# A spectral block with a 3x3 convolution: four rows from six products, a refined inverse root on GpSimd, a table of free PSUM banks and new order lists

## Chip, cores and metric

The kernel runs on one core of one Trainium2 chip. The metric is the device time of one execution in microseconds (us), as the median over runs. All data are fp32.

## What is computed

The input `x` is four images of 256 x 256 positions with 64 channels. Layer 0 normalises it over the channels, applies a spectral step (2-D FFT, a 256 x 256 mixing matrix with GELU, inverse FFT, projection), adds the result to `x`, and then does a second normalisation, a 64 to 128 projection, a depthwise 3x3 convolution, GELU and a 128 to 64 projection. Layer 1 replaces the sequence by its moving average plus a filtered rest, which the kernel does as one 256 x 256 matrix for each channel.

```python
h = _pw(_ln(x, g1, b1), w_te, b_te)
F = jnp.fft.fft2(h.astype(jnp.complex64), axes=(1, 2))
fr = jnp.concatenate([jnp.real(F), jnp.imag(F)], axis=-1)
fc = jax.nn.gelu(_pw(fr, w_fc, b_fc), approximate=False)
re, im = (fc[..., :HID], fc[..., HID:])
sp = jnp.real(jnp.fft.ifft2(re + 1j * im, axes=(1, 2)))
x1 = x + _pw(sp, w_tp, b_tp)
h2 = _pw(_ln(x1, g2, b2), w_fe, b_fe)
d = lax.conv_general_dilated(h2, w_dw, window_strides=(1, 1), padding='SAME',
                             dimension_numbers=('NHWC', 'HWIO', 'NHWC'), feature_group_count=HID) + b_dw
d = jax.nn.gelu(d, approximate=False)
return x1 + _pw(d, w_fp, b_fp)
```

## The kernel before

The kernel is one program with an order written out by hand for TensorE (PE), VectorE (DVE), ScalarE (ACT) and GpSimd (POOL). Every operation has a short name. Lists such as `FULL` and `SPECTRUM` say which operations one period `n` issues and for which index: `cf0:-3` is `cf0` for the chunk of three periods ago. `FOLLOWS` names what each operation needs before it, and `do` issues missing predecessors first. The queue SP holds nearly all DMAs, in an order that the framework derives.

There are five kinds of stages.

- The first (`FIRST`, `BETWEEN`) transforms columns of `x` along the height (`forward_h`) and builds layer 1's matrices.
- The second (`SPECTRUM`) goes on with the forward transform and does the spectral step, two pairs of frequency blocks in a period (`x`, `xs`, `m0`, `m1`, `gc`, `b`, `g`, `p`, `z`, `zs`, `w`, `zt`) and the inverse transform along the width (`u`, `us`, `uc`, `uf`).
- Then `FULL` adds one convolution chunk to each period. A chunk is 8 of 256 columns of one image, so there are 32 chunks for each image and 128 in all. While the forward transform still has chunks (it ends at period 127), such a period holds forward, spectral and convolution work. Later it holds spectral and convolution work, and for the last image convolution alone.
- Last comes layer 1, one 256 x 256 matrix product for each channel over all images (L1200), evicted by DVE and ACT in turns (L1214, L1212).

A convolution chunk goes like this. `s` finishes the inverse FFT (L833); `r0`, `r1` add it to `x` (L846, L853); `cq`, `cr`, `cR`, `cm`, `cM`, `cp` make the inverse norm (`statistics`, L192 to L233): the sum (L213), the squares on ACT (L210), minus the mean's square (L217), the sum of squares (L220), their sum (L224), and the power -1/2 on GpSimd (L230). `cx` scales (L237), `t` transposes to channels (L870), `tt` evicts (L878). `T0`, `T1` form sums of rows on GpSimd (L890 to L895): this is the fast algorithm for a 3-tap filter that gets two output rows from four products. `gm`, `gh` and `em`, `eh` make these products on PE: `wc_main` for two neighbouring columns at once (L916) and `wc_half` for the third (L935), into banks of 512 columns, one for each product and column parity. `gc_`, `cf`, `ce` put the products together into two rows (L955 to L967), `cE` corrects the image's edges (L974 to L980), `a` is the GELU (L984), `o` the projection (L991), `fs`, `ft`, `st` turn it back and add it to `x1` (L1002 to L1026).

PSUM banks come from one pool of eight in rotation (`bank`, L141): the n-th tile gets the bank of the tile eight places before it.

The lines that carry the algorithm for two rows:

```python
if i:
    even, odd = by_row(1)[:, 0], by_row(1)[:, 1]
    nc.gpsimd.tensor_tensor(td[:, 0], odd, even, ALU.add)
    nc.gpsimd.tensor_tensor(td[:, 1], odd, even, ALU.subtract)
    ks = (1, 2)
else:
    for r in range(2):
        nc.gpsimd.tensor_tensor(td[:, r], by_row(0)[:, r], by_row(2)[:, r], ALU.subtract)
    ks = (0, 3)
```

Of the kernel before, what the change touches and what calls it, by code (L numbers as in the profile page):

```python
# [11 lines left out]
F32 = mybir.dt.float32  # L12
AF = mybir.ActivationFunctionType
ALU = mybir.AluOpType
# [4 lines left out]
P = 128  # L19
N = 256  # L20
# [4 lines left out]
NPOS = float(N * N)  # L25

# [10 lines left out]
def _tables():  # L37
# [4 lines left out]
    fold = lambda m: m.reshape(2, P, -1).transpose(1, 0, 2).reshape(P, -1)  # L42

# [8 lines left out]
    ihi[0] = 0.5 * cos[P, :P] / NPOS  # L52

# [8 lines left out]
    icr[0] *= 0.5  # L62

# [5 lines left out]
    first = np.maximum(off_h, (dx == 0)[:, None])  # L69
    last = np.maximum(off_h, (dx == 2)[:, None])  # L70
    rows = off_h[:, [0, N - 1] * 4]
    edge = np.zeros((P, 2 * N + 8))
# [21 lines left out]
    for par in range(2):  # L94
# [20 lines left out]
        "avgT": fold(avg.T),  # L115
# [14 lines left out]
def conv_seq_kernel(ctx: ExitStack, tc: tile.TileContext, a: dict, tables: bass.AP, out: bass.AP):  # L130
# [5 lines left out]
    psum = ctx.enter_context(tc.tile_pool(name="psum", bufs=8, space=PSUM))  # L136
# [4 lines left out]
    def bank(name):  # L141
        return psum.tile([P, 512], F32, tag="bank", name=name)
# [42 lines left out]
    wc_main = const([P, 2, 4, HID], "wc_main")  # L185
    wc_half = const([P, 4, HID], "wc_half")
# [3 lines left out]
    edge_rows = const([P, 4, 2], "edge_rows")  # L190

    def statistics(pool, index, src, name):  # L192

        state = {}

        def get(j):
            if j not in state:
                n = src(j).shape[1]
                state[j] = [
                    pool.tile([P, n], F32, tag=tag, name=f"{tag}_{name(j)}", bufs=bufs)  # L200
                    for tag, bufs in (("total", 2), ("squares", 2), ("var", 3))
                ]
            return state[j]

        squares = {}

        def square(j):
            n = src(j).shape[1]
            squares[j] = shared.tile([P, n, C], F32, tag="sq", name=f"sq_{name(j)}")
            nc.scalar.activation(squares[j], src(j), AF.Square)  # L210

        def add(j):
            nc.vector.tensor_reduce(get(j)[0], src(j), AX.X, ALU.add)  # L213

        def less_mean(j):
            total, _, var = get(j)
            nc.vector.scalar_tensor_tensor(var, total, -1.0 / C, total, ALU.mult, ALU.mult)  # L217

        def add_squares(j):
            nc.vector.tensor_reduce(get(j)[1], squares.pop(j), AX.X, ALU.add)  # L220

        def variance(j):
            _, total, var = get(j)
# [147 lines left out]
    def forward_h(pool):  # L371
# [73 lines left out]
        def evict(j, m):  # L445
# [12 lines left out]
            if out[j] < 2:  # L458
                return
# [983 lines left out]
```

## Time and profile before

| | us |
|---|---|
| median of 3 runs | 4445.63 |
| lowest, highest | 4442.97, 4450.9 |
| span of the profiled execution | 4447.0 |
| granted TensorE clock, mean | 0.993 |
| DVE busy in that span | 3561.7 |
| GpSimd busy | 2774.3 |
| ScalarE busy | 2505.2 |

The profile counts from the first to the last instruction. Its page gives the busy time of each engine; the costliest groups by line, engine, operation and tile follow with count, busy time, mean time of one, and the idle time ahead of them. These are some of the groups:

```profile
L594 POOL TENSOR_TENSOR g<-g 128x512 f32<-128x512 f32 (+1 forms) x520 | 736.2, 1429 | 520.9 <-ACT g L588 520.9
L916 PE MATMUL ps_h_c<-td_c,wc_main 128*128 128x512 f32 x2048 | 921.7, 593 | 0.0
L230 POOL TENSOR_TENSOR rstd_c<-var_c,minus_half 128x16 f32<-128x16 f32 x128 | 371.8, 2905 | 468.1 <-DVE var_c L224 457.4
L935 PE MATMUL ps_h_c<-td_c,wc_half 64*128 64x128 f32 (+1 forms) x4032 | 515.3, 392 | 4.3 <-POOL td_c L890 4.3
L967 DVE TENSOR_TENSOR h_c<-h_c,ps_h_c 128x512 f32<-128x512 f32 x512 | 317.3, 682 | 125.8 <-PE ps_h_c L935 125.7
```

Busy time is a union, so a matmul's mean of 593 ns with 450 ns busy each means that neighbours overlap in the pipeline. The two passes of one fp32 product are counted as two instructions.

### The profile page before, as it was taken

Reading aid. Unit: us, or ns where it says so; the run is one execution under the profiler, and the core shown is the slowest. Engines: PE = TensorE matmul, PEld = TensorE weight load, DVE = VectorE, ACT = ScalarE, POOL = GpSimd, SP = SyncE. Lnnn points to the kernel's source line nnn. Section 1 sums busy time; section 2 is a strip of 40 time slices with the busy share of each in tenths; the row PEclk is TensorE's granted clock in tenths of the full one; section 3 lists DMA queues with packets and bytes.
Section 4 is the critical chain, followed back from the end, with each engine's and each line's share of the span. In section 5 each row is a group of like instructions: output and inputs, shape, how many; then the busy total and the mean of one; then the engine's idle time right before and its main releaser. Section 6 shows DMA issues by size and latency. Waiting matters only on the chain.

```text
span 4447.0 us, 63373 instructions
## 1 busy us (share of the span) xinstructions
PE 4346.2 (98%) x22379; PEld 2219.4 (50%) x22379; DVE 3561.7 (80%) x5473; ACT 2505.2 (56%) x3694; POOL 2774.3 (62%) x1774
## 2 busy tenths in 40 slices
PE   7899999799999999999999999999999999999999
PEld 4444443355555555455555555555555455554444
DVE  7979999899999999999998777777778788872222
ACT  2338888666666666666666666666664343431121
POOL 6869998887777777777777555555554555530000
PEclk9999999899999999999999999999999999999999
DMA  6665556444444444444444343333334433329996
GB/s 189 201 191 143 156 156 176 133 114 133 133 133 133 133 128 138 119 133 133 133 133 119 105 114 95 101 104 100 95 104 126 145 105 94 90 59 373 345 346 231
DMA packets 757733, 655.01 MB, mean 147 GB/s; under 512 B 40269, under 2 KB 651551, under 8 KB 749096
## 3 DMA queue, kind: packets, MB, share of 16 engines
q1 hardware_dynamic: 720552, 583.82, 44.3%
q10 hardware_dynamic: 36864, 67.13, 3.9%
q8 instruction: 179, 2.93, 0.3%
q14 instruction: 138, 1.13, 0.1%
HBM read 364.81 MB, written 286.00 MB: 146 GB/s over the span
## 4 chain that ended last, share of the span: by engine, by line
PE 88%; DVE 5%; POOL 2%; DMA 2%; issue 1%; ACT 1%; SPq 1%; ACTq 0%; DVEq 0%; POOLq 0%
PE ps_h_c L916 19%; PE ps_h_c L935 11%; PE ps_p L565 10%; PE ps_o L1200 9%; PE ps_z L618 5%; PE ps_u L667 5%; PE ps_f_c L991 5%; PE ps_x L541 5%; PE ps_s_c L833 5%; PE ps_y L436 4%; PE ps_ft_c L1012 3%; PE ps_t_c L870 3%; PE ps_zt L635 2%; DMA out_dram<-oc 1%; PE ps_m L1120 1%
## 5 line engine op out<-in xcount | busy, mean ns | idle before, releaser
L594 POOL TENSOR_TENSOR g<-g 128x512 f32<-128x512 f32 (+1 forms) x520 | 736.2, 1429 | 520.9 <-ACT g L588 520.9
L916 PE MATMUL ps_h_c<-td_c,wc_main 128*128 128x512 f32 x2048 | 921.7, 593 | 0.0
L584 DVE TENSOR_TENSOR g<-ps_p,g 128x512 f32<-128x512 f32 x1040 | 692.9, 682 | 30.4 <-ACT g L579 12.4
L588 ACT ACTIVATE g<-g,b_fc 128x1024 f32<-128x1024 f32 (+1 forms) x520 | 586.5, 1148 | 180.3 <-DVE g L584 177.8
L230 POOL TENSOR_TENSOR rstd_c<-var_c,minus_half 128x16 f32<-128x16 f32 x128 | 371.8, 2905 | 468.1 <-DVE var_c L224 457.4
L579 ACT COPY g<-ps_p 128x512 f32<-128x512 f32 (+1 forms) x520 | 302.0, 582 | 453.3 <-PE ps_p L565 438.8
L916 PEld LDWEIGHTS ps_h_c<-td_c,wc_main 128*128 128x128 f32 x2048 | 369.1, 190 | 369.8 <-issue 303.0
L935 PEld LDWEIGHTS ps_h_c<-td_c,wc_half 64*128 64x128 f32 x4032 | 417.0, 187 | 244.4 <-issue 194.4
L565 PE MATMUL ps_p<-xs,wp 64*128 64x512 f32 (+1 forms) x2080 | 519.0, 603 | 6.3 <-ACT xs L556 6.3
L935 PE MATMUL ps_h_c<-td_c,wc_half 64*128 64x128 f32 (+1 forms) x4032 | 515.3, 392 | 4.3 <-POOL td_c L890 4.3
L1200 PE MATMUL ps_o<-xc,mt 128*128 128x512 f32 x1024 | 439.9, 592 | 1.3 <-DVE oc L1214 1.3
L230 POOL TENSOR_TENSOR rstd<-var,minus_half 128x16 f32<-128x16 f32 x128 | 384.6, 3005 | 87.5 <-DVE var L224 87.5
L967 DVE TENSOR_TENSOR h_c<-h_c,ps_h_c 128x512 f32<-128x512 f32 x512 | 317.3, 682 | 125.8 <-PE ps_h_c L935 125.7
L984 ACT ACTIVATE h_c<-h_c,b_conv 128x1024 f32<-128x1024 f32 x256 | 280.7, 1147 | 200.6 <-DVE h_c L980 200.5
L1214 DVE TENSOR_SCALAR oc<-ps_o,b_fp 128x512 f32<-128x512 f32 x128 | 93.2, 749 | 345.4 <-DMA out_dram<-oc 181.1
L430 POOL TENSOR_TENSOR xb<-xt 128x512 f32<-128x512 f32 x224 | 288.3, 1305 | 91.9 <-DVE xt L423 89.9
L960 DVE TENSOR_TENSOR h_c<-h_c,ps_h_c 128x512 f32<-128x512 f32 x256 | 175.7, 686 | 202.0 <-PE ps_h_c L935 193.5
L1200 PEld LDWEIGHTS ps_o<-xc,mt 128*128 128x128 f32 x1024 | 194.4, 190 | 246.1 <-issue 236.1
L541 PEld LDWEIGHTS ps_x<-tab,yb 128*64 128x64 f32 x4064 | 241.9, 138 | 129.8 <-issue 91.6
L618 PE MATMUL ps_z<-g,w_tp 128*64 128x512 f32 x1024 | 281.9, 613 | 22.2 <-POOL g L594 21.0
L1212 ACT ACTIVATE oc<-ps_o,b_fp 128x512 f32<-128x512 f32 x128 | 85.9, 686 | 356.6 <-PE ps_o L1200 171.0
L436 PE MATMUL ps_y<-xb,tab 128*64 128x512 f32 x1024 | 257.1, 609 | 28.8 <-POOL xb L430 28.0
(144 smaller groups left out, 7676.8 us busy)
## 6 DMA issues: line engine op xcount, KB each, us to landing
y_d<-yt SPq DMA_DIRECT2D x256, 256.0 KB, 2.5
yb<-y_d SPq DMA_DIRECT2D x256, 256.0 KB, 3.7
u_d<-ut SPq DMA_DIRECT2D x256, 256.0 KB, 4.1
x_c<-in_x_dram SPq DMA_DIRECT2D x128, 512.0 KB, 5.6
x_d<-st SPq DMA_DIRECT2D x128, 512.0 KB, 4.8
xc<-x_d SPq DMA_DIRECT2D x64, 1024.0 KB, 8.6
out_dram<-oc ACTq DMA_DIRECT2D x256, 256.0 KB, 6.0
xt<-in_x_dram SPq DMA_DIRECT2D x504, 128.0 KB, 2.7
```

The source lines that it names most:

```text
L230: nc.gpsimd.tensor_tensor(rstd, var, minus_half.to_broadcast([P, n]), ALU.pow)
L436: nc.tensor.matmul(ps[i * C : (i + 1) * C], dh[:, m, i * C : (i + 1) * C], sums[j][:, i], start=True, stop=True,)
L541: nc.tensor.matmul(ps[r * C : (r + 1) * C, j * N + t * P : j * N + (t + 1) * P], blk[:, t, k, r * C : (r + 1) * C], tb[:, t, :], start=Tru ...
L565: nc.tensor.matmul(ps[:, :nf], wp[rows, cols], rhs[rows], start=True, stop=r == 1 or not pr["special"],)
L584: nc.vector.tensor_tensor(gt[:, i], re, gt[:, 1], op)
L588: nc.scalar.activation(g, g, AF.Gelu, bias=b_fc[:, half : half + 1])
L594: nc.gpsimd.tensor_tensor(g[:, 0], g[:, 0], g[:, 1], op)
L618: nc.tensor.matmul(ps[r * C : (r + 1) * C, :nf], w_tp, d[:, :nf], start=True, stop=True)
L916: nc.tensor.matmul(ps, wc_main[:, par, k, :], ts[(*j, k)].rearrange("p j i -> p (j i)"), start=True, stop=False,)
L935: nc.tensor.matmul(pss[k, par][:, s * P : (s + n) * P], wc_half[lo : lo + C, k, :], ts[(*at_q, k)][lo : lo + C, at : at + n, :].rearrange( ...
L967: nc.vector.tensor_tensor(g, g, m, (ALU.add, ALU.subtract)[r])
L1200: nc.tensor.matmul(ps[:, :nf], mts[i // CM][:, i % CM, t, to * P : (to + 1) * P], xc[:, t, :, :, i, :], start=t == 0, stop=t == 1,)
```

## The change

Six things change together.

1. The convolution gets four output rows from six products in place of two rows from four. The rows of a chunk lie in four planes of 64 (row modulo 4). `tt` is evicted three times, as it is, times 4 and times 2 for two planes; GpSimd forms six inputs (`row_sums`); each product has 256 columns in place of 512. Products 3 and 4 of both parities share a pair of banks of their own. The three ring slots of `td` lie next to each other, and `around` copies the end columns so that every `wc_half` product is one instruction.
2. Putting together: `evict_first`, `combine_first` (DVE, with sums written back to PSUM), and products 0 and 5 either evicted by ACT and added by GpSimd (`evict_rest`, `add_sums`, with the edge rows) or, for the last 33 chunks (`is_late`), added by DVE (`combine_rest`). `edges` keeps the columns alone.
3. The statistics: the mean's square is made by ACT and put beside the squares as a 65th column, the constant as a 66th, so that one reduce gives the variance. For the convolution the power on GpSimd becomes a seed by DVE (a multiply and add on the bits as an integer) and ten small GpSimd operations that refine it. In `FULL` periods the forward chunk's norm is refined together with the convolution's, 32 columns in place of 16.
4. PSUM: a list of free banks; `free` after the last reader puts a bank back, and the next tile takes the one that came free first. Six banks from the convolution on, as two are the pair. `make_room` issues the releasing operation earlier where no bank is free.
5. `x` for the convolution is loaded by four DMAs of 32 partitions (row modulo 4); `uc` and `st` have one buffer in place of two.
6. New lists: `FULL` while the forward transform runs, `MIXED` with spectral work, `CONV` for the last image, and new `FIRST` and `SPECTRUM`.

The core of the diff:

```diff
+    def bank(name, keep=True):
+
+        at = free_banks.pop(0)
+        if keep:
+            taken[name] = at, busy[-1]
+        else:
+            free_banks.append(at)
+        pool = psum if at < BANKS else psum2
+        return pool.tile([P, 512], F32, tag=f"bank{at}", name=name)
...
         def less_mean(j):
-            total, _, var = get(j)
-            nc.vector.scalar_tensor_tensor(var, total, -1.0 / C, total, ALU.mult, ALU.mult)
+            mean = shared.tile([P, ROWS, 1], F32, tag="mean", name=f"mean_{name(j)}", bufs=2)
+            total = get(j)["total"][:, own].unsqueeze(2)
+            nc.scalar.activation(mean, total, AF.Square, scale=float(C) ** -0.5)
+            nc.scalar.mul(sq[:, :, C : C + 1], mean, -1.0)
...
+                nc.vector.tensor_scalar(
+                    seed.bitcast(I32), var.bitcast(I32), -0.5, float(0x5F3759DF), ALU.mult, ALU.add
+                )
...
+            tt(t0, seed, seed, ALU.mult)
+            tt(t0, t0, var, ALU.mult)
+            ts(t0, t0, -0.5, 1.5, ALU.mult, ALU.add)
+            tt(rstd, t0, seed, ALU.mult)
+
+            tt(t0, rstd, rstd, ALU.mult)
+            tt(t0, t0, var, ALU.mult)
+            ts(t1, t0, 0.375, -1.25, ALU.mult, ALU.add)
+            tt(t1, t1, t0, ALU.mult)
+            ts(t1, t1, 1.875, None, ALU.add)
+            tt(rstd, t1, rstd, ALU.mult)
...
+            src = x[b, :, q * W : (q + 1) * W, :].rearrange("(t i r) w c -> r i t (w c)", t=2, r=4)
+            for r in range(4):
+                nc.sync.dma_start(
+                    x1s[j][r * 32 : (r + 1) * 32].rearrange("p t w c -> p t (w c)"), src[r]
+                )
...
+            nc.scalar.copy(tt[:, ONE : ONE + 4, js, 0:Q], ps)
+            nc.scalar.mul(tt[:, FOUR : FOUR + 4, js, 1 : Q + 1], ps, 4.0)
+            nc.scalar.mul(tt[:, TWO : TWO + 2, js, 0:Q], ps[:, 0:4:2], 2.0)
...
+            if i == 0:
+                tt_(a_nb, plane(ONE + 3, 0, ONE + 2, 0), a_nb, ALU.subtract)
+                tt_(c_e, c_e, plane(ONE + 1, 0, TWO, 0), ALU.subtract)
+                a_c, nb_e = plane(FOUR + 1, 1, ONE + 3, 0), plane(FOUR, 1, TWO + 1, 0)
+                for k, op in ((1, ALU.add), (2, ALU.subtract)):
+                    tt_(new[:, k : k + 3 : 2], a_c, nb_e, op)
             else:
+                p_q = plane(ONE + 1, 0, FOUR + 2, 1)
+                tt_(p_q, plane(FOUR + 3, 0, FOUR + 2, 1), plane(ONE + 1, 0, ONE, 1), ALU.subtract)
+                tt_(new[:, 0:6:5], a_nb, p_q, ALU.add)
...
+            for k in ks:
+                for par in range(2):
+                    nc.tensor.matmul(
+                        product(j, k, par),
+                        wc_main[:, par, k, :],
+                        td[:, k, slots(j)].rearrange("p j q -> p (j q)"),
+                        start=k in (0, 1, 3),
+                        stop=False,
                     )
...
+                for par in range(2):
+                    two = product(j, 2, par)
+                    tt_(s[:, 0, par], s[:, 1, par], two, ALU.add)
+                    tt_(s[:, 1, par], s[:, 1, par], two, ALU.subtract)
+                    free(f"ps_h_{name(j)}_1_{par}")
+            else:
+                g = planes_of(j)
+                three, four = banks[j][2][:, :, 0:256], banks[j][2][:, :, 256:512]
+                tt_(three, g[:, 1], four, ALU.add)
+                tt_(four, g[:, 1], four, ALU.subtract)
+                first, last = (s[:, 0], s[:, 1]) if is_late(j) else (g[:, 0], g[:, 3])
+                tt_(g[:, 0], three, first, ALU.add)
+                stt(g[:, 2], three, 4.0, s[:, 0], ALU.mult, ALU.add)
+                stt(g[:, 3], four, 8.0, last, ALU.mult, ALU.add)
+                stt(g[:, 1], four, 2.0, s[:, 1], ALU.mult, ALU.add)
...
+        if any(n - k in chunk_at for k in range(7)):
+            names = FULL if n < B * FWD + 4 else MIXED if n < CONV_FROM else CONV
         else:
             names = SPECTRUM
+        joint["on"] = names is FULL
```

## The prediction

> **What bounds the kernel now.** I read the busy shares first, then the same shares stage by stage, then the order in time inside one period of each stage.
>
> ```profile
> PE 4346.2 (98%) x22379; PEld 2219.4 (50%) x22379; DVE 3561.7 (80%) x5473; ACT 2505.2 (56%) x3694; POOL 2774.3 (62%) x1774
> ...
> 1100.00:1200.00 100.00, 100.00 (x580) 52.46 (x577) 95.48 (x146) 66.90 (x100) 79.62 (x51) 1.00 0.45 128
> 2700.00:2800.00 100.00, 100.00 (x586) 53.78 (x583) 78.56 (x126) 65.52 (x96) 51.33 (x40) 1.00 0.38 106
> 3600.00:3700.00 100.00, 100.00 (x486) 54.35 (x485) 84.42 (x129) 40.05 (x55) 52.88 (x36) 1.00 0.34 103
> ```
>
> The last three lines are windows of 100 us (PE, PEld, DVE, ACT, POOL busy, then clock, DMA). PE is full in all three conv stages, so PE is the bound there. The reader should see the second column of cover: DVE is at 95% in the first stage, at 79% in the second and 84% in the third.
>
> The length of a period comes from the timeline: two issues of the same load in the first stage, two in the second, and PE's blocks in the third.
>
> ```profile
> 1502.17 0.92 SPq L496 DMA_DIRECT2D yb<-y_d  x2
> 1529.90 0.92 SPq L496 DMA_DIRECT2D yb<-y_d  x2
> ...
> 2704.28 0.92 SPq L496 DMA_DIRECT2D yb<-y_d  x2
> 2730.29 0.91 SPq L496 DMA_DIRECT2D yb<-y_d  x2
> ...
> 3599.88 3.60 PE L916 MATMUL ps_h_c<-td_c,wc_main 128*128 128x512 f32 x8
> 3603.41 2.00 PE L935 MATMUL ps_h_c<-td_c,wc_half 64*128 64x128 f32 x16
> 3605.35 1.09 PE L1012 MATMUL ps_ft_c<-ident,fs_c 128*128 128x128 f32 x8
> 3606.28 3.60 PE L916 MATMUL ps_h_c<-td_c,wc_main 128*128 128x512 f32 x8
> 3609.80 2.00 PE L935 MATMUL ps_h_c<-td_c,wc_half 64*128 64x128 f32 x16
> 3611.64 1.88 PE L833 MATMUL ps_s_c<-uc_c,tab 64*128 64x512 f32 x8
> ...
> 3616.26 3.60 PE L916 MATMUL ps_h_c<-td_c,wc_main 128*128 128x512 f32 x8
> ```
>
> So a period is 27.73 us with the forward stage (61 periods by the code, 60 chunks), 26.01 us with the spectral stage alone (38 periods, 37 chunks), 16.38 us with the convolution alone (31 chunks). From start to next start, the products of a chunk take 3.53 + 3.52 = 7.05 us in wc_main and 1.94 + 1.84 = 3.78 us in wc_half. Before about 800 us nothing of the convolution runs, and the last 447 us are layer 1; I leave both as they are.
>
> **What the Trainium skill says.** "SBUF — State Buffer", section "Who interferes with whom": a DVE instruction with two SBUF inputs contends with a GpSimd instruction that reads SBUF, a tensor_scalar may too, and the loser blocks for the whole instruction. The trace agrees: with GpSimd near 80% the two-SBUF update of ut takes far longer than with GpSimd at half load.
>
> ```profile
> L716 DVE SCALAR_TENSOR_TENSOR ut<-ut,ut 128x1024 f32<-128x1024 f32 x13 | 26.7, 2057 | 0.0
> ...
> L716 DVE SCALAR_TENSOR_TENSOR ut<-ut,ut 128x1024 f32<-128x1024 f32 x15 | 18.1, 1208 | 0.0
> ...
> L322 DVE TENSOR_SCALAR w_mid<-w_dwb 128x384 f32<-128x384 f32 x1 | 2.1, 2102 | 0.0
> ```
>
> (1000 to 1700 us, 2500 to 3300 us, and the whole run.) "GPSIMD Engine Reference", sections "Instruction dispatch" and "Elementwise": every instruction pays a software dispatch and a join of eight cores, and two inputs share a read port. The trace gives 1.04 us at 512 elements (L891) and 1.90 us at 1024 (L237): 1.68 ns an element and 0.18 us fixed. "TensorE: Matmul & The Clock Gate", section "LDWEIGHTS": a load's time goes with its columns, not its rows. The trace agrees (190 ns with 128 rows, 187 with 64).
>
> **The change part by part.**
>
> *TensorE.* Each fp32 product is two passes. Before: 16 passes of 512 columns in wc_main per chunk; after: 6 products, two parities, so 24 passes of 256. A pass of 256 with 128 x 128 weights is in the trace already:
>
> ```profile
> 255.46 3.72 PE L1120 MATMUL ps_m<-t,vs 128*128 128x256 f32 x16
> 259.02 1.02 PE L1109 MATMUL ps_v<-t,w 128*128 128x512 f32 x2
> ```
>
> 16 passes in 3.56 us, 0.2225 us each, so the 190 ns load still hides. 24 x 0.2225 = 5.34 us, 1.71 us less. The wc_half passes run in two row groups side by side: 12 slots of 0.2225 = 2.67 us plus about 0.12 us of fill for each of the two blocks, 2.91 us, 0.87 us less. Together 2.6 us a chunk. PE's periods become 25.1, 23.4 and 13.8 us.
>
> *DVE, first stage.* Busy before: 0.952 x 27.73 = 26.4 us. The two edge adds go (0.96 us in the timeline). The four small variance operations go (about 0.6). The reduces grow from 64 to 66 columns (+0.08). The joint seed is one small tensor_scalar (+0.2 if free, up to 2 if it is blocked as L322 was). The combination was 2.66 + 2.40 = 5.06 us from start to start; now it is four operations of 256 (L1163: 405 ns, 0.36 from start to start) and six of 512 at 0.66: 1.45 + 3.98 = 5.43 (+0.37). Writing back to PSUM is not in the trace; I price it as reading. Sum: 25.5 us, above PE's 25.1.
>
> *DVE, second stage:* 0.773 x 26.01 = 20.1; nearly the same trades give 19.9, which is 85% of 23.4. *Third stage:* 16.38 less the waits before L967 and L960 (0.92 + 1.33) is 14.1. Edge adds there took 1.75 with their blocking and go; variance -0.3; seed +0.2; reduce +0.04; combination +0.38. These chunks are the late ones: GpSimd adds nothing for them and DVE gets two row-edge operations (about 0.3 each, between the 0.16 and 0.5 that an edge add took) and two adds of 512 (0.66): +1.9. Sum 14.6, above PE's 13.8.
>
> *ScalarE.* Per chunk: the second and third writing of tt 2 x (0.59 + 0.37) = 1.92, the rest's eviction 1.18, first eviction +0.2, the two small operations of less_mean 0.44 for each norm (L464: 0.215), around 0.3. First stage 18.4 to 22.9 us, second 16.3 to 20.4: below PE's, by little.
>
> *GpSimd.* First stage 0.797 x 27.73 = 22.1. Both powers go (2 x 2.9). Row sums grow from four to six operations (+2.1), add_sums brings two of 512 and two small ones (+2.6). The refinement is ten dependent operations on 32 columns: by the line above 0.23 us each, with the waits between them I take 0.3, 3.0 in all. Sum 24.0. Second stage: 13.8 - 2.9 + 2.1 + 2.6 + 2.8 = 18.4. The third needs about 11.
>
> *Queues, banks, statistics.* The load of x becomes four DMAs instead of one: three more issues of 0.47 us on SP, which waits most of the time, and they are queued behind the spill of u as the single one was. Six banks with a pair replace eight: the pair is held from the products to the end of cf1, which the lists put within one period. The other cover (stats joined, lists reordered) has no cost of its own. The tail's pipeline is one period deeper: +5 us.
>
> *Sum.* First stage: DVE's 25.5 plus a blocked seed or ut now and then and a little waiting, 26.5 us: 1.2 less, x 60 = 72. Second: PE's 23.4 plus 0.3, so 2.3 x 37 = 85. Third: 14.6 plus 0.6, 15.2, so 1.2 x 31 = 37. 72 + 85 + 37 - 5 = 189. The profiled execution's 4447.0 becomes 4258. It stood 1.4 us above the median of the runs, so 4257.
>
> **Rivals.** *PE stays the bound throughout.* For it: before, PE was at 100% with DVE at 95%, so a list can pack this closely. Against it: the sums for DVE. 2.6 x 128 = 333, less the tail: 4118.
>
> *Contention eats the first stage.* With GpSimd at 24.0 of 26.5 us, the seed, ut, xb and xt operations on DVE find the port taken more often; 1.2 us more in a period returns it to 27.7. Then 74 from the second stage, nothing from the first and third: 4377.
>
> *Slower: the refinement makes GpSimd the bound.* Each of the ten operations waits for the one ahead, and behind them on GpSimd stand xn's scaling, which TensorE's transposes wait for, and the four folds, which ps_z waits for. At 0.3 us each GpSimd needs 24.0; every 0.1 us adds 1.0 us. It passes 27.7 at 0.67 us each. The total passes zero at about 0.85 us each: 29.5 us a period, 1.8 x 60 = 108 lost, against 2.1 x 37 + 37 - 5 = 110 from the other stages. At 0.9 us it is 30.0 us: +136, the second stage at 24.4 gains 59, the third 37: about 4490. Against it: small GpSimd memsets take 0.1 us; for it: nothing of 32 columns with such waits is in the trace.
>
> *The change does nothing measurable:* only where the cases meet.
>
> **How the numbers follow.** The forecast 4257 has 56% (its own range 4190 to 4320), PE throughout 18%, contention 13%, GpSimd as bound 11%, no change 2%. Within 0.2% (9 us) is what a measurement can't tell from no change. Faster: 56 + 18 + 13 = 87%; same 2%; slower 11%. The range reaches 4115 at the bottom and 4385 at the top; the slow case and the tails left out are some 20%.
>
> **What would show it.** wc_main at 0.22 us a pass and 24 a chunk; periods of 26.5, 23.7 and 15.2 us; DVE at 96% or more in the first and third stage with PE below 97%, PE at 98% or more in the second; the refinement's operations at 0.2 to 0.35 us. The prediction is wrong if PE is full in the first and third stage (then DVE was priced too high), if GpSimd is above 97% in the first, or if a stage before 800 us moves by more than 10 us.

## The result and the profile after

The changed kernel takes 4368.82 us (median of four runs, 4367.59 to 4370.57), the kernel before 4446.18 in the runs beside it. The ratio is 0.982 with a 95% interval of 0.9806 to 0.9834. It is faster by 77 us; the forecast was 189. The profiled execution has a span of 4368.8 us (4447.0 before) and a mean granted clock of 0.985 (0.993 before).

The same three windows of 100 us as in the prediction, for the changed kernel (PE, PEld, DVE, ACT, POOL busy, then clock, DMA share, GB/s):

```profile
1100.00:1200.00 100.00, 98.63 (x590) 52.25 (x588) 92.49 (x135) 79.58 (x144) 95.87 (x100) 1.00 0.48 137
...
2800.00:2900.00 100.00, 100.00 (x655) 63.84 (x651) 84.04 (x132) 83.65 (x145) 83.37 (x107) 1.00 0.40 107
...
3600.00:3700.00 100.00, 100.00 (x581) 68.12 (x582) 96.91 (x173) 62.83 (x121) 83.94 (x121) 1.00 0.42 117
```

GpSimd went from 80% to 96% in the first stage, and TensorE is full in the two others. The timeline of TensorE gives the periods, as the distance of two starts of ps_s, the first product of a chunk (start, us, line, tiles; two lines for each stage):

```profile
1326.29 1.99 PE L983 MATMUL ps_s_c<-uc_c,tab 64*128 64x512 f32 x8
1353.95 1.99 PE L983 MATMUL ps_s_c<-uc_c,tab 64*128 64x512 f32 x8
...
2841.19 1.91 PE L983 MATMUL ps_s_c<-uc_c,tab 64*128 64x512 f32 x8
2864.76 1.91 PE L983 MATMUL ps_s_c<-uc_c,tab 64*128 64x512 f32 x8
...
3607.47 1.88 PE L983 MATMUL ps_s_c<-uc_c,tab 64*128 64x512 f32 x8
3621.27 1.88 PE L983 MATMUL ps_s_c<-uc_c,tab 64*128 64x512 f32 x8
```

So a period is 27.66 us in the first stage (27.73 before), 23.57 in the second (26.01), about 13.9 in the third, this one 13.80 (16.38). The starts of ps_s over all 128 chunks show where the changed kernel gets ahead and where it falls back:

| chunk | start before | start after | after is ahead by |
|---|---|---|---|
| 5 | 957.6 | 966.1 | -8.5 |
| 26 | 1540.0 | 1547.6 | -7.7 |
| 57 | 2426.4 | 2443.3 | -16.9 |
| 72 | 2816.7 | 2817.6 | -0.9 |
| 93 | 3362.9 | 3311.2 | 51.8 |
| 101 | 3513.4 | 3496.2 | 17.2 |
| 127 | 3939.1 | 3857.3 | 81.8 |

Inside the stages it gains 0.07 x 60 + 2.44 x 37 + 2.5 x 31 = 172 us. Some 94 us go elsewhere: 8 ahead of the first chunks, 9 around the image boundary of the first stage, some 20 up to chunk 72 (15 chunks at 2.44 would have brought 37, and 16 came), 54 between chunks 93 and 101, where some 20 should have come and 35 were lost, and 4 at the end. By the starts of ps_s the step across an image boundary (chunks 31 to 32, 63 to 64, 95 to 96) grew by 6, 7 and 14 us. Two questions follow: why does the first stage gain nothing, and what do the transitions cost?

### The profile page after: what moved, and what is told of

The parts are those of the page before. It is cut to its first block, busy times and chain, and to the rows that moved or that the text cites. A ratio compares the mean times of both kernels' runs of the same rounds, so it can differ in the third digit from the quotient of the medians.

```text
span 4368.8 us, 67589 instructions
## 1 busy us (share of the span) xinstructions
PE 4183.0 (96%) x22443; PEld 2308.1 (53%) x22443; DVE 3453.4 (79%) x5227; ACT 2892.5 (66%) x5121; POOL 3315.0 (76%) x3509
## 4 chain that ended last, share of the span: by engine, by line
PE 78%; DVE 9%; POOL 4%; ACT 4%; DMA 3%; issue 2%; SPq 1%; DVEq 0%; POOLq 0%; ACTq 0%
PE ps_p L692 10%; PE ps_o L1446 10%; PE ps_h_c L1108 9%; PE ps_h_c L1122 5%; PE ps_x L667 5%; PE ps_f_c L1225 5%; PE ps_u L798 5%; PE ps_s_c L983 5%; PE ps_y L557 4%; PE ps_z L747 4%; PE ps_hh_c L1108 4%; PE ps_zt L765 3%; PE ps_t_c L1030 3%; PE ps_ft_c L1250 2%; PE ps_hh_c L1122 2%
## 5 line engine op out<-in xcount | busy, mean ns | idle before, releaser
L723 POOL TENSOR_TENSOR g<-g 128x512 f32<-128x512 f32 (+1 forms) x520 | 677.0, 1313 | 126.3 <-ACT g L717 115.9
L692 PE MATMUL ps_p<-xs,wp 64*128 64x512 f32 (+1 forms) x2080 | 566.5, 616 | 13.1 <-ACT xs L682 7.2
L1108 PE MATMUL ps_h_c<-td,wc_main 128*128 128x256 f32 x2048 | 506.8, 390 | 0.7 <-ACT zs L755 0.3
L1108 PEld LDWEIGHTS ps_h_c<-td,wc_main 128*128 128x128 f32 x2048 | 369.7, 192 | 143.2 <-ACT h_c L1142 41.4
L1070 POOL TENSOR_TENSOR td<-tt 128x512 f32<-128x512 f32 x256 | 324.6, 1290 | 10.0
L1122 PE MATMUL ps_h_c<-td,wc_half 64*128 64x256 f32 (+1 forms) x2048 | 293.2, 401 | 2.4 <-POOL td L1074 1.0
L1264 DVE TENSOR_TENSOR st<-x_c,ps_ft_c 128x256 f32<-128x256 f32 x512 | 259.8, 596 | 40.4 <-PE ps_ft_c L1250 40.4
L1225 PE MATMUL ps_f_c<-h_c,w_fp 128*64 128x512 f32 x1024 | 273.7, 621 | 15.8 <-ACT h_c L1218 14.6
L983 PE MATMUL ps_s_c<-uc_c,tab 64*128 64x512 f32 x1024 | 260.8, 622 | 21.5 <-DVE uc_c L932 13.3
L692 PEld LDWEIGHTS ps_p<-xs,wp 64*128 64x128 f32 x2080 | 185.1, 186 | 182.1 <-issue 67.8
```

Of the source, the lines that this page charges most:

```text
L692: nc.tensor.matmul(ps[:, :nf], wp[rows, cols], rhs[rows], start=True, stop=r == 1 or not pr["special"],)
L723: nc.gpsimd.tensor_tensor(g[:, 0], g[:, 0], g[:, 1], op)
L983: nc.tensor.matmul(pss[i], tb[i * C : (i + 1) * C], uc[i * C : (i + 1) * C, ::-1, 1 - r, :] if down else uc[i * C : (i + 1) * C, :, r, :], ...
L1108: nc.tensor.matmul(product(j, k, par), wc_main[:, par, k, :], td[:, k, slots(j)].rearrange("p j q -> p (j q)"), start=k in (0, 1, 3), stop ...
L1122: nc.tensor.matmul(product(j, k, par)[:, dst.start * Q : dst.stop * Q], wc_half[lo : lo + C, k, :], td[lo : lo + C, k, src].rearrange("p j ...
L1225: nc.tensor.matmul(ps[par * C : (par + 1) * C], w_fp, gs[j][:, :, par, i0 : i0 + 2, :].rearrange("p r j q -> p r (j q)"), start=True, stop ...
```

## The experiments

For each run the median, its ratio to the kernel before with the 95% interval, and the mean period of the first stage (chunks 8 to 24, by the starts of ps_s); the changed kernel has 4368.82 us and 27.66 us.

| run | what | us | ratio | first stage |
|---|---|---|---|---|
| e1 | shorter refinement | 4407.07 | 0.9891 to 0.992 | 28.13 |
| e2 | DVE operation twice | 4383.42 | 0.9838 to 0.9871 | 27.72 |
| e3 | GpSimd operation twice | 4446.65 | 0.9986 to 1.0004 | 29.16 |
| e4 | convolution a period later | 4373.82 | 0.9818 to 0.9847 | 27.66 |
| e5 | ps_s halved | 4368.08 | 0.9804 to 0.9834 | 27.79 |
| e6 | e1 and e5 | 4381.8 | 0.9836 to 0.9869 | 27.93 |
| e7 | blocks joined | 4376.45 | 0.9821 to 0.9857 | 27.60 |
| e8 | e1 and e7 | 4477.72 | 1.0047 to 1.0077 | 29.63 |
| e9 | power for refinement | 4380.24 | 0.9826 to 0.9859 | 28.21 |
| e10 | layer 1's loads later | 4373.03 | 0.9814 to 0.9844 | |
| e11 | CONV one period earlier | 4374.25 | 0.9813 to 0.9843 | |
| e12 | CONV two periods earlier | 4389.29 | 0.9851 to 0.988 | |
| e13 | a fold on DVE | 4405.34 | 0.9884 to 0.9914 | 28.28 |
| e14 | a row sum left out | 4392.12 | 0.9848 to 0.9881 | 28.12 |
| e15 | no refinement | 4403.59 | 0.9881 to 0.991 | 28.10 |
| e16 | scaling earlier | 4367.22 | 0.9798 to 0.9827 | |
| e17 | shapes apart in MIXED | 4420.4 | 0.9917 to 0.995 | |
| e18 | e6 and no update of ut | 4365.91 | 0.9801 to 0.983 | 27.67 |

### Is GpSimd the bound of the first stage?

e1 takes work from GpSimd, e2 gives DVE more, e3 gives GpSimd more.

```diff
# e1
-            ts(t0, t0, -0.5, 1.5, ALU.mult, ALU.add)
-            tt(rstd, t0, seed, ALU.mult)
-            tt(t0, rstd, rstd, ALU.mult)
-            tt(t0, t0, var, ALU.mult)
...
-            tt(rstd, t1, rstd, ALU.mult)
+            tt(rstd, t1, seed, ALU.mult)
# e2
                 stt(g[:, 2], three, 4.0, s[:, 0], ALU.mult, ALU.add)
+                if joint["on"]:
+                    stt(g[:, 2], three, 4.0, s[:, 0], ALU.mult, ALU.add)
# e3
                 tt_(new[:, 0:6:5], a_nb, p_q, ALU.add)
+                if joint["on"]:
+                    tt_(new[:, 0:6:5], a_nb, p_q, ALU.add)
```

> The refinement on GpSimd is six operations in place of ten: the first (Newton) step is left out, and the cubic step starts from the seed, so the norm is less exact. Nothing else changes. Theory A (in the first convolution stage GpSimd is the bound: 26.4 us busy of a period of 27.67 and a small gap ahead of each dependent operation): the four operations left out took, in the trace of the changed kernel, 1.12 for the first of the chain or about 0.6 for each of the next, some 1.6 us in a period with their gaps; 60 periods give 95 us, down to 4275, and at most 140 us if the longer operations go. DVE then comes up to 97% and takes over near 26 us. The periods of the second stage (PE full, 23.57) and third (13.87) stay. Rival B (DVE is the bound, as the prediction had it, or the contention between DVE and GpSimd): the period stays within 0.3 us of 27.67, the total within 20 us of 4369.

> One DVE operation of the combination (4 x three + s, 512 columns, about 0.67 us) is issued twice in each period of the first convolution stage; the result is the same value again. Theory A (GpSimd is the bound there): DVE has about 2 us of room in 27.67, so the period grows by 0.2 us or less and the total by less than 12 us. Rival B (DVE is the bound): 0.67 us x 60 = 40 us more.

> One of GpSimd's six row sums (the one that makes two planes, 1.28 us in the trace of the changed kernel) is issued twice in each period of the first convolution stage, with the same value again. Theory A (GpSimd is the bound there): 1.28 + 0.08 us more in a period, x 60 = about 80 us more. Rival B (DVE is the bound, GpSimd has room): less than 20 us more. Both bounds at once would show as an increase here and in the run with the doubled DVE operation.

The doubled GpSimd operation costs more than its own 1.28 us (1.5 us a period, 78 us in all), the doubled DVE operation 0.06 us in a period and 15 us in all; in its profiled execution the first stage is 9 us longer, 8 of them around the image boundary. Yet with less to do for GpSimd the kernel is 38 us slower. So GpSimd has no room for more, but it doesn't alone set the period. Theory A falls as it was put, and so does rival B, which allowed 20 us for e1.

The refinement did cost more than was priced. Groups of GpSimd for the changed kernel, in 1100 to 1500 us and then in 2800 to 3000 us (count, busy, mean ns, idle ahead):

```profile
L337 POOL TENSOR_SCALAR newton_c<-newton_c 128x32 f32<-128x32 f32 x14 | 15.3, 1091 | 1.2
...
L337 POOL TENSOR_SCALAR newton_c<-newton_c 128x16 f32<-128x16 f32 x8 | 1.6, 206 | 0.7
```

The same operation, the slowest of the ten in the first stage, takes 0.2 us where GpSimd has time and 1.1 us there. That it has twice the columns is not the reason: in e1 it takes 0.22 us at 32 columns, and most of the operations that are left 0.22 to 0.29. The timeline of the changed kernel shows what stands beside it:

```profile
1316.41 1.22 DVE L849 SCALAR_TENSOR_TENSOR ut<-ut,ut 128x1024 f32<-128x1024 f32 x1
1316.45 1.24 POOL L337 TENSOR_SCALAR newton_c<-newton_c 128x32 f32<-128x32 f32 x1
```

It lasts as long as DVE's update of ut in place, which began just before it.

### GpSimd relieved in other places

e13 gives one fold to DVE, e14 leaves out a row sum, e15 leaves out nine of ten refinement operations, each in the first stage alone. e9 puts the power back.

```diff
# e13
+            engine = nc.gpsimd
+            if joint["on"] and half == 1 and prs.index(pr) % 2 == 0:
+                engine = nc.vector
-            nc.gpsimd.tensor_tensor(g[:, 0], g[:, 0], g[:, 1], op)
+            engine.tensor_tensor(g[:, 0], g[:, 0], g[:, 1], op)
# e14
-                tt_(c_e, c_e, plane(ONE + 1, 0, TWO, 0), ALU.subtract)
+                if not joint["on"]:
+                    tt_(c_e, c_e, plane(ONE + 1, 0, TWO, 0), ALU.subtract)
# e15
+            if joint["on"]:
+                ts(rstd, seed, 1.0, None, ALU.mult)
+                return
# e9
-            if alone or not side:
+            if True:
                 nc.gpsimd.tensor_tensor(rstd, var, minus_half.to_broadcast([P, n]), ALU.pow)
```

> In the periods of the first convolution stage one of GpSimd's four folds (g, 1.28 us) is done by DVE, one add of 512 columns (0.69 us by the same shape in the trace); the work is the same. Theory A (GpSimd's queue holds the first stage, and the run with the short refinement gained nothing only because its freed time put other operations of DVE and GpSimd beside each other): GpSimd needs 26.3 us, DVE 26.1, the period falls to about 26.8: 0.5 to 0.9 us x 60 = 30 to 55 us less. Theory B (the three engines' queues wait for each other, any shift costs as much as it brings): within 15 us of 4369, or slower.

> In the periods of the first convolution stage one of GpSimd's six row sums (1.28 us) is left out, so the products work on other numbers; nothing is put in its place. Theory A: 1.36 us less on GpSimd, DVE (25.4 us busy and about a microsecond of waiting for ScalarE) takes over at 26.5: 1.1 us x 60 = 65 us less. Theory B: within 15 us of 4369, as the short refinement.

> In the periods of the first convolution stage nine of the ten operations of the refinement are left out (the seed is used as it is, so the norm is off by a few per cent); the others keep theirs. GpSimd needs about 22.2 us there. Theory A: the period falls to DVE's 26.5, which is the period that the prediction gave: 1.2 x 60 = 70 us less. Theory B: the period stays above 27.3, because DVE and GpSimd block each other elsewhere or TensorE's chain of blocks (27.3 busy) holds it.

> The power -1/2 on GpSimd (one operation for each norm, 16 columns) in place of the seed on DVE and the ten small operations, everywhere; all else as in the changed kernel. Before the change that power took 2.9 us. Theory R (the refinement brings nothing: in the first stage its ten operations take 4.97 us and some 0.8 us of gaps, two powers take 5.8; in the second and third stage ten operations of 0.22 us with gaps take about 3.0, one power 2.9): within 20 us of 4369. Theory Q (the refinement is worth what the prediction put on it, 2.8 us of GpSimd in each period of the first stage): with GpSimd as the bound there, 60 to 160 us more. If DVE's blocked seed (0.74 us in the first stage) matters: up to 40 us less.

Three reliefs, which take 0.8 to 3.2 us of GpSimd's busy time from a period, give mean periods of 28.1 to 28.3 us, all longer than with no relief. Theory A, which wanted 30 to 70 us less, falls. Theory B has the direction, though e14, slower by 23 us, is beyond its 15. What they have in common is seen in the groups; first the changed kernel, then e15 (both 1100 to 1500 us):

```profile
L352 POOL TENSOR_TENSOR xn_c<-x_c,rstd_c 128x1024 f32<-128x1024 f32 x15 | 28.6, 1904 | 0.0
...
L849 DVE SCALAR_TENSOR_TENSOR ut<-ut,ut 128x1024 f32<-128x1024 f32 x7 | 8.4, 1203 | 0.0
```

```profile
L355 POOL TENSOR_TENSOR xn_c<-x_c,rstd_c 128x1024 f32<-128x1024 f32 x15 | 40.6, 2706 | 0.0
...
L852 DVE SCALAR_TENSOR_TENSOR ut<-ut,ut 128x1024 f32<-128x1024 f32 x8 | 13.3, 1658 | 0.0
```

With GpSimd earlier, the scaling xn and DVE's update of ut are both longer, by 0.8 and 0.45 us (e13 has 2.85 and 1.42). They then stand side by side, as here in e1:

```profile
1322.17 1.43 DVE L844 SCALAR_TENSOR_TENSOR ut<-ut,ut 128x1024 f32<-128x1024 f32 x1
1322.48 2.88 POOL L347 TENSOR_TENSOR xn_c<-x_c,rstd_c 128x1024 f32<-128x1024 f32 x1
```

In the changed kernel xn starts 2 us or more after ut has ended (chunks 8 to 25), and a small refinement operation takes the delay in its place. So the freed time is partly paid to two larger operations. Nor is every period longer: by the starts of ps_s, e1, e14 and e15 repeat 27.48, 27.67 and 29.0 us, and in the third the update of ut, one in a period, takes 2.03 us. The Trainium skill says in "SBUF — State Buffer", section "Who interferes with whom", that a DVE instruction with two inputs in SBUF contends with a GpSimd instruction that reads SBUF; the lines agree. In e18 below, without the ut updates, xn has 2.03 us, and the periods of 29.04 us that e6, with them, still has are gone. How much of those was the blocking and how much DVE's load isn't shown.

The power (e9) costs 11 us against the refinement. One power over 32 columns takes 5.87 us, as long as the ten operations (5.0) with their gaps (0.8). So the refinement, priced at 2.8 us less in each first-stage period, brings 0.55 of them between chunks 8 and 24, and nothing between chunks 38 and 54, where both periods are 27.67 us.

### TensorE's share

e5 halves ps_s, e6 adds e1, e7 joins blocks of TensorE in FULL, e8 adds e1 to that. e17 does the reverse of e7 in MIXED, where TensorE is full.

```diff
# e5
-            for r, tb in enumerate((ihr, ihi)):
+            for r, tb in enumerate((ihr,) if joint["on"] else (ihr, ihi)):
...
-                        stop=r == 1,
+                        stop=r == 1 or joint["on"],
# e7, in FULL
-  t0:-2 tt0:-2 fl ... ul t1:-2 s ... o1:-5 x:3 ... o0:-5 p1 ... y0:-2 yt0:-2 ... y1:-2 yt1:-2
+  fl ... ul t0:-2 t1:-2 tt0:-2 s ... o1:-5 o0:-5 x:3 ... p1 ... y0:-2 y1:-2 yt0:-2 ... yt1:-2
# e17, in MIXED
-  r0 gc_1:-4 m0 gc0 m0:1 ... x:2 b0 xs:2 o1:-5 fs1:-5 u:-1
+  r0 gc_1:-4 x:2 m0 gc0 o1:-5 m0:1 ... b0 xs:2 fs1:-5 u:-1
```

> In the periods of the first convolution stage the last step of the inverse FFT (ps_s) leaves out one of the two products that it accumulates: 4 passes of 512 columns in place of 8 on TensorE, about 0.86 us less in a period; nothing else changes. Theory C (TensorE and GpSimd end together there: TensorE's chain of blocks fills 27.67 us, and GpSimd needs 27.6 with its gaps): GpSimd holds the period, the total changes by less than 15 us. Theory D (TensorE alone is the bound, since the run with less work on GpSimd gained nothing): 0.86 x 60 = 52 us less, about 4317.

> Both cuts: the halved ps_s and the refinement of six operations (its first step left out). Theory C: only with both does the first stage get shorter: against the run with the short refinement alone (4407) 0.5 to 0.86 us in a period, 30 to 52 us less, unless DVE, which was at 91% and met longer blocked operations in that run, holds it. Theory D: the same gain as the halved ps_s alone has against the changed kernel (52 us). If DVE's blocked operations are the bound once GpSimd has room: within 15 us of 4407.

> Only the list FULL changes: the two halves of t, of o and of y stand next to each other, so that TensorE has 22 blocks in a period in place of 25 (before the change: 18); the work is the same. Theory S (each change of block costs TensorE 0.1 to 0.25 us, and the list's finer blocks took back most of the 2.3 us that the six products save): TensorE's own time in a period falls by 0.4 to 0.6 us, seen as idle time on TensorE if GpSimd holds the period; the total changes by less than 15 us. Rival (a matmul's time doesn't depend on the blocks around it, the longer steps of p, f and y have another cause): the steps from start to start of these blocks stay as they are.

> The joined blocks and the refinement of six operations (its first step left out). Theory C with S: with room on GpSimd the shorter TensorE chain counts: 0.4 to 0.6 us in a period against the run with the short refinement alone (4407), 24 to 36 us less. If DVE's blocked operations are the bound in that run: within 15 us of 4407.

> Only the order on TensorE in MIXED changes: the block of ps_x stands between ps_s and the first half of ps_p, one block of ps_f between the two halves of ps_p; before they stood with blocks of their own shape. The work is the same. In a period there are 10 places in place of 6 where the shape of the stationary operand changes (64 rows x 128 columns, 128 x 64, 128 x 128). Theory S (each such change costs TensorE some 0.19 us, as the weights then don't load beside the products ahead; the list FULL has 18 of them where the list of before had 6, which is 2.3 us and eats what the six products save): TensorE is the bound in this stage, so 4 x 0.19 = 0.76 us in each of some 34 periods, 26 us more, the period 23.57 becoming 24.3. Rival (the longer steps in the first stage are waits for other engines): within 5 us of 4369.

Less work for TensorE alone gains nothing (e5), with GpSimd relieved too it gains 25 us against e1, less than theory C asked for, and none against the changed kernel (e6). Joined blocks alone cost 8 us (e7). With e1 they cost 71 us more than e1 (e8), which neither theory had: the joined blocks make ps_u wait 2.0 us in a period for DVE's s_c. TensorE's timeline in MIXED shows the price of a change of shape, first the changed kernel, then e17 (start, modelled length, tiles, rows x columns of the stationary operand):

```profile
2841.19 1.91 PE L983 MATMUL ps_s_c<-uc_c,tab 64*128 64x512 f32 x8
2842.91 1.90 PE L692 MATMUL ps_p<-xs,wp 64*128 64x512 f32 x8
2844.80 1.08 PE L747 MATMUL ps_z<-g,w_tp 128*64 128x512 f32 x4
2845.68 1.07 PE L667 MATMUL ps_x<-tab,yb 128*64 128x128 f32 x16
2846.55 1.06 PE L1225 MATMUL ps_f_c<-h_c,w_fp 128*64 128x512 f32 x4
2847.43 1.90 PE L798 MATMUL ps_u<-zt,tab 128*64 128x512 f32 x8
```

```profile
2910.45 1.91 PE L983 MATMUL ps_s_c<-uc_c,tab 64*128 64x512 f32 x8
2912.28 1.09 PE L667 MATMUL ps_x<-tab,yb 128*64 128x128 f32 x16
2913.31 1.13 PE L692 MATMUL ps_p<-xs,wp 64*128 64x512 f32 x4
2914.37 1.08 PE L1225 MATMUL ps_f_c<-h_c,w_fp 128*64 128x512 f32 x4
2915.38 1.13 PE L692 MATMUL ps_p<-xs,wp 64*128 64x512 f32 x4
2916.43 1.08 PE L747 MATMUL ps_z<-g,w_tp 128*64 128x512 f32 x4
2918.18 1.94 PE L798 MATMUL ps_u<-zt,tab 128*64 128x512 f32 x8 [0.67 <-ACT g L706]
```

From ps_s to ps_u it was 6.24 us and is 7.73. In e17 ps_u starts 1.75 us after ps_z, where such a block takes 0.88: 0.87 us are a new wait for g. The other 0.62 us stand for four more changes of shape: 0.155 us each. The period is 1.55 us longer, of which 0.62 are the changes and the rest nearly all the wait. The expectation had the changes alone, 26 us; 52 came. Blocks of one shape show no such cost: from ps_z to ps_x, to ps_f_c and to ps_u the changed kernel takes 0.87 to 0.88 us a block, which is four passes of 0.216 (a block of eight passes of ps_hh_c takes 1.73).

The weight loads of the changed kernel show the difference. Between 1100 and 1500 us the first load of a block starts 0.2 to 0.4 us ahead of the first product where the shape stays (but for one ps_x in each period, whose load waits for DVE's x_c), and no more than 0.03 us ahead of it at each of the 233 changes without a wait.

Counted in the order of the weight loads, FULL has 17 changes of shape in a period where the kernel before had 6; MIXED has 6 and CONV 5. That makes 11 x 0.155 = 1.7 us of TensorE's time in each first-stage period, an estimate from e17, of the 2.6 that the six products were to save.

### What holds 27.67 us

e18 takes away something from all three engines in the first stage: e5, e1 and DVE's in-place updates of ut.

```diff
# e18, beside e5 and e1
-                nc.vector.scalar_tensor_tensor(
-                    flat(even), flat(even), 2.0, flat(sums), ALU.mult, ALU.subtract
-                )
+                if not joint["on"]:
+                    nc.vector.scalar_tensor_tensor(
+                        flat(even), flat(even), 2.0, flat(sums), ALU.mult, ALU.subtract
+                    )
...
-                nc.vector.tensor_tensor(flat(odd), flat(even), flat(odd), ALU.add)
+                if not joint["on"]:
+                    nc.vector.tensor_tensor(flat(odd), flat(even), flat(odd), ALU.add)
```

> In the periods of the first convolution stage three things are left out together: one of the two products of ps_s (TensorE, 0.86 us), the first step of the refinement (GpSimd, some 1.6 us), and the update of ut in place (DVE, 1.2 us, 1.6 us where it is blocked; once in a period). Against the run with the first two (4382): Theory E (three queues of nearly the same length hold the stage, and DVE with its blocked operations is the one left): the period falls from 27.93 to 26.8 or less, 1.1 x 60 = 66 us less, about 4316. Rival (the coupling of the queues, not any length, holds it near 27.9): within 15 us of 4382.

The period is 27.67 us again, with TensorE at 96%, DVE at 88% and GpSimd at 86%. Then no engine's load sets it. Theory E, which wanted 26.8 us or less, falls; of the rival, the coupling of the queues is left. The chain of waits of e18 over one period shows what does (start, us, what):

```profile
1271.24 1.09 PE ps_x L662 x16
...
1290.49 0.92 PE ps_p L687 x4
...
1291.48 0.54 ACT g L701
...
1293.82 0.95 ACT sq L275
1294.77 0.48 ACT us L810
...
1295.28 0.44 DVE ut L824
...
1297.72 1.14 DVE x_c L993
...
1298.90 1.09 PE ps_x L662 x16
```

It is a loop through three queues: TensorE's blocks from ps_x to ps_p, with one round through ACT on the way (20.2 us), then ACT from g to us (3.8), then DVE from ut to x_c (3.6), and then ps_x again, which starts 0.04 us after x_c, the last reader of a bank of ps_s. From start to start it is 27.66 us. Neither half of ps_s, nor the refinement, nor the updates in place (ut<-ut,ut) lie on it; the ut of the chain is the add from ps_u. In the timeline of the changed kernel the same points stand as close (ps_p, g, us, ut, x_c, ps_x):

```profile
1322.29 1.02 PE L692 MATMUL ps_p<-xs,wp 64*128 64x512 f32 x4
...
1323.45 0.59 ACT L706 COPY g<-ps_p 128x512 f32<-128x512 f32 x1
...
1326.59 0.62 ACT L815 COPY us<-ps_u 128x512 f32<-128x512 f32 x1
...
1327.24 0.69 DVE L829 TENSOR_TENSOR ut<-ps_u,us 128x512 f32<-128x512 f32 x1 [0.63 <-ACT us L815]
...
1329.61 1.21 DVE L996 TENSOR_TENSOR x_c<-x_c,ps_s_c 128x1024 f32<-128x1024 f32 x1
...
1330.87 1.09 PE L667 MATMUL ps_x<-tab,yb 128*64 128x128 f32 x16
```

The reader sees that x_c ends at 1330.82 and ps_x starts at 1330.87: the hand-over that the chain of e18 names is as tight here, though the page counts no idle time for TensorE there, since a matmul's modelled end covers it. The three parts have the same lengths in both kernels, 20.2, 3.8 and 3.6 us. In all 35 periods of the changed kernel that were measured (chunks 8 to 25 and 38 to 54) ps_x starts 0.05 to 0.06 us after x_c, and ut 0.03 us after us. So the order in the list FULL makes a loop of 27.67 us, and it holds the period in the changed kernel too.

The next limits are close behind. In one period of three of e1, e14 and e15, x_c ends 0.6 us ahead of ps_x, and nearly all of these periods take 27.48 us. So an order that shortens the loop alone (us ahead of sq on ACT, say) would bring about 0.2 us a period, 12 us over 60: an estimate, as no such order was tried. In e7, which has another order, x_c ends 1.3 to 1.5 us ahead of ps_x, and the period is still 27.60: there the loop doesn't hold it, and what does was not shown. GpSimd has no room either (e3). The loop, TensorE's order and GpSimd with its gaps lie within some 0.2 us of each other.

### The transitions

```diff
# e4
-    LATE = 0
+    LATE = 1
# e10
-            mts = [matrix_load(seq, c) for c in range(0, CG, CM)]
-            xc = x2_load(seq, 0, 0, 1)
...
+                if n == S0 + LATE + opened(B - 1) + 2 + 4:
+                    mts = [matrix_load(seq, c) for c in range(0, CG, CM)]
+                    xc = x2_load(seq, 0, 0, 1)
# e11 and e12
-    CONV_FROM = S0 + LATE + opened(B - 1) + 3
+    CONV_FROM = S0 + LATE + opened(B - 1) + 3 - 1    # e12: - 2
# e16
+    moved = ("cx", -1)
+    ENDING = [w for w in MIXED if w != moved]
+    ENDING.insert(ENDING.index(("T0", -2)), moved)
...
-            names = FULL if n < B * FWD + 4 else MIXED if n < CONV_FROM else CONV
+            names = FULL if n < B * FWD + 4 else MIXED if n < S0 + 129 else ENDING if n < CONV_FROM else CONV
```

> All convolution chunks are placed one period later against the spectral work (LATE = 1); the work is the same. Theory T (at the start, at the image boundaries and at the change to the last image the period that the chunk is in waits for spectral results that the new lists want too early: about 90 us in all): the gap ahead of the first chunk of each image shrinks by up to 20 us each, and one more period is paid at the end (13.9 us at the third stage's rate) or one spectral period more ahead of the first chunk: 20 to 60 us less in all. Rival U (the losses come from what must be drained and filled at a change of lists, whatever the placement): the gaps stay and the extra period costs 10 to 30 us.

> Layer 1's first loads (four matrices and the first 4 MB of x1) are issued four periods later; nothing else changes. At the change to the last image they stand on SP ahead of the loads of u for the second chunk, which took 16.1 us there. Theory L (this transfer is what delays the chunks 97 and 98): 8 to 14 us less. Rival (GpSimd's and ScalarE's chain through that stretch is the bound, the transfer lies beside it): within 4 us of 4369.

> The list CONV takes over from MIXED one period earlier. In the last four periods of MIXED the spectral front is already done, and they still take 22 to 23 us, with TensorE waiting 3 us for the scaled xn behind GpSimd's sums (the convolution alone takes 13.9 in CONV). Theory M (the order of MIXED without spectral work is what is slow there): 5 to 9 us less. Rival (the chain from the last spectral block to the next image's first chunk is as long in any order): within 4 us.

> CONV takes over two periods earlier. Theory M: 10 to 18 us less. Rival: within 4 us, or slower, if the spectral operations that are left are then issued late, all at once, ahead of the last image's first chunk.

> In the last six periods of MIXED, where the spectral front is done, the scaling xn (cx) stands on GpSimd ahead of the six row sums and not behind them; the work is the same. Theory M2 (there a loop through GpSimd, row sums, scaling, TensorE's transposes and products, holds the period at 22 to 23 us, and TensorE's clock falls after each wait): the period falls by 2 to 4 us, 10 to 20 us less in all. Rival (the spectral chain that is left, or the loads, hold it): within 4 us.

None of them recovers what its first theory wanted: e16 gains 1.6 us, which is within the spread of its runs, e4, e10 and e11 cost 4 to 5, and e12 costs 20. With the later start (e4) the 7.6 us that chunk 64 waits for uc in the changed kernel are made up, but the first chunk comes 9 us later. Counted from chunk 93, with the later loads (e10) chunk 97 comes 4 us earlier and chunk 98 is 4 late. With the scaling earlier (e16) chunk 96 comes 6 us earlier, and from chunk 98 on fewer than 3 are left of them. Each time most of the gain is gone again within a few chunks. Windows of 50 us at the last transition, first the kernel before, then the changed one:

```profile
3350.00:3400.00 50.00, 50.00 (x254) 25.60 (x250) 41.75 (x66) 26.85 (x38) 26.77 (x20) 1.00 0.27 74
3400.00:3450.00 50.00, 50.00 (x244) 27.14 (x245) 38.94 (x63) 18.37 (x26) 19.87 (x14) 1.00 0.64 203
3450.00:3500.00 50.00, 44.01 (x181) 21.45 (x180) 36.37 (x65) 16.34 (x24) 26.67 (x18) 0.93 0.59 197
```

```profile
3350.00:3400.00 50.00, 40.12 (x187) 27.58 (x185) 26.18 (x41) 20.88 (x39) 28.83 (x42) 0.86 0.32 82
3400.00:3450.00 50.00, 36.88 (x186) 21.87 (x184) 33.93 (x61) 19.02 (x37) 21.86 (x37) 0.93 0.78 258
3450.00:3500.00 50.00, 38.22 (x189) 24.94 (x189) 36.17 (x60) 22.79 (x44) 36.67 (x54) 0.86 0.28 78
```

TensorE waits 35 us of these 150 (6 before), and the clock granted is lower. What a wait does to the block after it is seen in the timeline of the changed kernel:

```profile
3392.96 1.11 PE L1030 MATMUL ps_t_c<-ident,xn_c 128*128 128x128 f32 x4 [3.75 <-POOL xn_c L352]
3393.87 3.62 PE L1108 MATMUL ps_h_c<-td,wc_main 128*128 128x256 f32 x8
```

A block of eight passes that takes 1.9 us elsewhere takes 3.6 after the wait. In the trace its passes start 0.427 us apart, those of the next blocks from 3398.5 on 0.216, and the granted clock is 0.50 from 3391.6 to 3398.4 and 1.00 after that. What exactly the 54 us are made of stays open: the waits are for GpSimd's xn, for uc and for the GELU in turn, and the slower clock adds to them. Between 3347 and 3491 us the clock is at 0.50 for 37.6 us in all (6.8 before), so by an estimate from these stretches it accounts for 19 us at most.

## Why the prediction was wrong

- **The step that failed in the first stage** is the one from the sums to the period: "First stage: DVE's 25.5 plus a blocked seed or ut now and then and a little waiting, 26.5 us". DVE's load was right (25.4 us, 92% of 27.66). But a period isn't the largest load plus a microsecond. The list FULL makes a loop of 27.67 us through TensorE, ACT and DVE, for which the prediction had no term, and the first stage gained 0.07 us in place of 1.2: 68 us of the difference. By size the other step that failed is the term for the transitions, below: 89 us.
- **TensorE's 25.1 us** left out the order. The products became shorter as priced (0.216 us a pass against 0.2225), but the list changes the shape 17 times in a period and not 6, at 0.155 us each by e17. The order of both kernels was there to be read. With the loop out of the way the periods seen in e1 still take 27.48 us, so 26.5 would not have come without the loop either; of these 2.4 us above 25.1 the changes of shape are an estimated 1.7, and the rest is not assigned.
- **GpSimd's 24.0 us** was 26.4 busy and some 27.6 with gaps. The refinement took 5.0 and not 3.0, five of the six row sums and the two sums 1.28 and not 1.05. e3 shows that GpSimd had no room left; the slower rival had the mechanism, but at 0.5 us an operation it stayed below the point from which it decides.
- **The second stage** was right: TensorE is the bound, 2.44 us in a period against 2.3.
- **The third stage** had DVE too dear: it is at 97% of 13.9 us, 13.4 and not 14.6, so TensorE, at 100%, is the bound by the profile (no run tested this stage alone), and the gain is 2.5, not 1.2; 40 us to the good.
- **The transitions** had 5 us in the sum and cost some 94. That the new lists may cost time at each boundary and change of list had no term of its own; what the 94 us are made of was not settled, beyond the waits and the slower clock shown above.

Together: 189 - 68 + 5 + 40 - 89 = 77 us; the two spans differ by 78. The rival of contention came nearest in time (4377), in good part by luck: it gave the third stage nothing, which gained 78 us, and the transitions 5 us of cost, which took 94, and these two errors nearly cancel. A part of its mechanism is there: the first stage gains nothing, and blocked operations belong to the reason that relief didn't help.

## What to carry to other kernels

With a hand-written order, work out the period as the longest loop through the engines' queues, not only as the largest sum of an engine; where several engines stand above 90%, taking work from one of them can even cost, as it did here with GpSimd. Count how often TensorE's order changes the shape of its weights, and keep blocks of one shape together. Price what a new order does at its beginning, its end and each boundary on its own: here that was 94 us against 172 gained inside the stages.

## What was not expected of the hardware

- A change of the stationary operand's shape cost TensorE 0.155 us (e17), where neighbouring blocks of one shape cost none. At a change the first load starts with its first product, elsewhere 0.2 to 0.4 us ahead of it (first stage of the changed kernel).
- Small GpSimd operations of 16 columns take 0.21 to 0.25 us with 0.08 us between dependent ones, and one of 32 columns that takes 0.22 us in e1 took 1.24 us beside a DVE update with two inputs in SBUF. A power over 32 columns takes 5.87 us; one over 16 took 2.9 in the kernel before and 3.9 in the second stage of e9.
- DVE adds of 512 columns that write back to PSUM take 0.70 us, those that only read there 0.68 to 0.69.
- In windows of 50 us with 10 to 13 us of waiting TensorE's granted clock was 0.86 to 0.93; while it stood at 0.50, passes started 0.427 us apart in place of 0.216.
